# Sparse graph attention, four layers: another place for the sums of the weights and for the outputs of a block

## The chip, the cores and the metric

The kernel runs on one core of one Trainium2 chip. The metric is the device time of one execution in microseconds. The kernel before took 2802.78 us, the median of three runs (2800.01 to 2805.45).

The core's engines work side by side, each through its own instructions in order: TensorE (PE; its weight loads are listed apart as PEld), VectorE (DVE), ScalarE (ACT), GpSimd (POOL) and SyncE (SP). They wait for each other on semaphores. Transfers run on 16 DMA engines.

## The reference, cut to what matters

There are 8 batches of 2048 nodes with 128 features, and one adjacency matrix in which a node has some 16 neighbours. Layers 0 and 1 are attention with 8 heads of 16 features over the neighbours, an output projection, a layer norm, a feed-forward part and a second layer norm. Layers 2 and 3 are graph attention with one score for each pair.

```python
scores = jnp.einsum('bnhd,bmhd->bhnm', Q, K) / sqrt(HEAD_DIM)
attn = softmax(where(adj == 0, -inf, scores))          # layers 0 and 1
x = layer_norm(h + einsum('bhnm,bmhd->bnhd', attn, V) @ Wo + bo)
x = layer_norm(x + relu(x @ W1 + b1) @ W2 + b2)
...
e = leaky_relu(s_i[:, :, None] + s_j[:, None, :])      # layers 2 and 3
x = layer_norm(softmax(where(adj == 0, -inf, e)) @ h + x)
```

The change touches layers 0 and 1 alone. The softmax is computed there as a sum of exponentials times values (the accumulator) and a sum of the exponentials themselves; the division comes at the end of a block.

## The kernel before, in words

**Blocks and chunks.** The nodes are sorted by their number of neighbours and cut into 16 blocks of 128. Block t has at most `CAPS[t]` neighbours for each node, from 29 down to 10. All 8 batches are done at once. In layers 0 and 1 a chunk is two neighbours of all 128 nodes (one, where the number is odd), so a block has between 15 and 5 chunks. A chunk's rows (keys and values of 8 batches, 8 KB for each neighbour) are gathered by indirect DMA (line 302, issued by POOL, up to five chunks ahead) into one of seven buffers `kv`.

**One attention chunk** (`attention_chunk`, lines 629 to 683) is a generator with these steps:

1. DVE multiplies the keys by the query (L637).
2. DVE adds the two halves of that product (L643); PE transposes and sums it into scores (L316, tile `pair`); ACT takes the exponential (L659, tile `ring`).
3. PE transposes it back (L663) and ACT copies it as the weights (L667). For the last chunk of a block PE also sums all of the block's exponentials (`block_sums`, L616 and L621) and ACT copies the sums (`partial`, L626).
4. DVE multiplies the values by the weights (L675).
5. PE adds the first neighbour's product into the accumulator `acc` (L316), 8 matmuls.
6. The same for the second neighbour.

**The order of the work** is written out by hand in `layers` (lines 1243 to 1304). Iteration i does step 3 of chunk i-1 and step 6 of chunk i-3; steps 1 and 2 of chunk i, each followed by a `slot`; then `weigh`, which does steps 4 and 5 of chunk i-2; and a third slot. So DVE's order in one iteration is L637 of chunk i, slot, L643 of chunk i, slot, L675 of chunk i-2, slot. At the change from layer 1 to layer 2 all chunks that are still open are weighed in the first iteration of layer 2.

**A slot** advances every generator in `threads` by one step, then every one in `tails`, and issues further gathers if their conditions hold. From layer 1 on, while a layer's input table isn't complete, it advances the tails twice.

**The end of a block.** In `weigh`, when the chunk is the block's last, `sums` (L685 to L697) runs: DVE adds the two halves of the partial sums (L688, 128x64), ACT takes the logarithm (L690), and a thread `scales` is added, in which ACT takes the exponential of minus the logarithm (L710, 128x1024), PE transposes it in two halves in the next two slots (L719, recorded as L316 with tile `m`), and ACT copies each half into the tile `scale` (L721). For a layer's last block DVE also reduces all sums to a minimum and a maximum there (L694, L695). One iteration later, after step 6 of the last chunk, the thread `tail` (L1206) is added: it waits some slots, then `outputs` (L699 to L703) lets DVE multiply the accumulator by the scale in two halves into the tile `o`. After that two generators `attention_tail` (L728) are added to `tails`, one for each half of the batches: the output projection (L739, L743), layer norm (L483, L490), feed-forward part (L756, L761, L768, L773), second layer norm, and the projection of the next layer's rows (L520, L526 or L530). A whole tail takes 21 steps. It ends in `state_done` (L545): the block's state is stored and a later one loaded (SP, L551 and L298), and the rows are scattered into the next layer's table (POOL, L507). Gathers of the next layer wait for these scatters; the first two blocks of a layer have their neighbours sorted so that their first chunks don't need the last three blocks.

In layer 0 there is besides a thread `find_lists` for each block, started in the first iteration of the block two before: its DVE part (MAX8 and MATCH_REPLACE8, lines 361 to 398) makes the neighbour list of a block.

Of the kernel before, what the change touches and what calls it, by code (L numbers as in the profile page):

```python
# [20 lines left out]
NT = N // P  # L21
# [68 lines left out]
def sparse_path(ctx: ExitStack, tc: tile.TileContext, ins: dict, out: bass.AP, flag: bass.AP):  # L90
# [365 lines left out]
    def reciprocal_sums(l, t, w, columns, folded):  # L456

        sums = small.tile([P, columns], F32, tag="sums", name="sums")
        n = CAPS[t] if t > 0 else BASE
        nc.vector.tensor_reduce(  # L460
            sums, w[:, :n, :].rearrange("p s c -> p c s"), axis=AX.X, op=ALU.add
        )
        if t == 0:
            nc.vector.tensor_add(sums, sums, folded)
        nc.vector.tensor_reduce(dmin[:, l, t : t + 1], sums, axis=AX.X, op=ALU.min)
        nc.vector.tensor_reduce(dmax[:, l, t : t + 1], sums, axis=AX.X, op=ALU.max)
        nc.vector.reciprocal(sums, sums)
        return sums
# [216 lines left out]
    def sums(l, t, box):  # L685
        if l < 2:
            both = box["partial"]
            nc.vector.tensor_add(block_sum[:, t, :], both[:, : NB * NH], both[:, NB * NH :])  # L688
            box["r"] = small.tile([P, NB * NH], F32, tag="logs", name="logs", bufs=1)
            nc.scalar.activation(box["r"], block_sum[:, t, :], AF.Ln)  # L690
            threads.append(scales(l, box))
            if t == NT - 1:
                every = block_sum.rearrange("p t c -> p (t c)")
                nc.vector.tensor_reduce(dmin[:, l, :1], every, axis=AX.X, op=ALU.min)  # L694
                nc.vector.tensor_reduce(dmax[:, l, :1], every, axis=AX.X, op=ALU.max)  # L695
            return
        box["r"] = reciprocal_sums(l, t, box["w"], NB, box.get("folded"))  # L697

    def outputs(l, t, box):  # L699
        acc, scale = box["acc"], box["scale"]  # L700
        box["o"] = o = work.tile([P, NB, P], F32, tag="o", name="o", bufs=1)
        for i in range(0, NB, 4):
            nc.vector.tensor_mul(o[:, i : i + 4, :], acc[:, i : i + 4, :], scale[:, i : i + 4, :])  # L703

    def scales(l, box):

        box["scale"] = scale = work.tile([P, NB, P], F32, tag="oT", name="scale", bufs=1)
        if l < 2:
            r = box["r"].rearrange("p (b h) -> p b h", h=NH)
            nc.scalar.activation(  # L710
                scale.rearrange("p b (j h) -> p b j h", h=NH),
                r[:, :, None, :].to_broadcast([P, NB, HD, NH]), AF.Exp, scale=-1.0,
            )
            yield
        for i in range(0, NB, 4):
            pt = misc()
            for j in range(4):
                r = box["r"][:, i + j : i + j + 1].to_broadcast([P, P])
                turn_into(pt[:, j * P : (j + 1) * P], scale[:, i + j, :] if l < 2 else r, j == 0)  # L719
            yield  # L720
            nc.scalar.copy(scale[:, i : i + 4, :].rearrange("p b n -> p (b n)"), pt)  # L721
# [479 lines left out]
    def later(n, make):  # L1201
        for _ in range(n):
            yield
        yield from make()

    def tail(l, t, box):  # L1206
        for _ in range(4 if l < 2 else 3 if t > NT - 4 else 5):
            yield
        outputs(l, t, box)
        if l < 2:  # L1210
            tails.append(later(1, lambda: attention_tail(l, t, box, 0)))
            tails.append(later(4, lambda: attention_tail(l, t, box, 4)))
        else:
            tails.append(later(1, lambda: gat_tail(l, t, box)))
        yield
# [14 lines left out]
    def go(c, times=1):  # L1230

        for _ in range(times if c["l"] is not None else 0):
            next(c["run"], None)

    def weigh(some, added):

        for c2 in some:
            if c2["last"]:
                sums(c2["l"], c2["t"], c2["box"])
            go(c2, 2)  # L1240
            added.append(c2)

    def layers():
# [7 lines left out]
        for i in range(len(every) + 2):  # L1251
# [3 lines left out]
            while added:  # L1255
                c2 = added.pop(0)
                go(c2)
                if c2["last"]:
                    threads.append(tail(c2["l"], c2["t"], c2["box"]))
# [23 lines left out]
            if c["l"] not in (0, 1) and weighed:  # L1283
                weigh(weighed, added)
                weighed = []
# [9 lines left out]
            if len(weighed) > 2:  # L1295
                weigh(weighed[:1], added)
                weighed.pop(0)
            if c1["l"] in (2, 3):
                go(c1, 2)
                if c1["last"]:  # L1300
                    threads.append(tail(c1["l"], c1["t"], c1["box"]))
# [533 lines left out]
```

## Time and profile before

| what | value |
|---|---|
| runs | 2802.78 us median (2800.01 to 2805.45) |
| the profiled execution's own time | 2808.35 us |
| its span | 2806.6 us |
| granted TensorE clock, mean | 0.937 |
| busy: PE / PEld / DVE / ACT / POOL | 84% / 76% / 90% / 49% / 63% |
| DMA | 982 MB, 350 GB/s; gathers take 82% of 16 engines' span |
| attention layers (first gathered chunk to the entry of layer 2) | 245 to 1893 us of the span |
| L637, L643, L675 for two neighbours | 2.28, 1.22, 2.28 us |
| L688, pair of L703 | 0.22, 1.28 us |

The span runs from the first to the last recorded instruction; the own time is some 1.75 us longer. A row of the timeline gives the start (us), the duration (us), the engine, the line, the operation, the tile written and the tiles read with their shape, how many instructions were merged, and in brackets how long the engine had been idle and which instruction released it. In the list of waits the columns are the waiting engine, tile and line, what it waited for, the total in us, the number of times and the longest. Where a helper records every operation, all have one line: L316 is every transpose and every value sum, and the tile tells which (`pair` scores, `acc` values, `m` the rest).

### The profile page before, as it was taken

What the parts mean: (1) busy time and instruction counts of PE and PEld (TensorE: products, weight loads), DVE (VectorE), ACT (ScalarE), POOL (GpSimd) and SP (SyncE); (2) the same over time, 40 slices, a digit from 0 to 9 for tenths busy, and PEclk for the clock granted to TensorE, in tenths of its full rate; (3) what the DMA queues carried; (4) which work ended last, traced back from release to release, by engine and by line L of the source; (5) the groups of instructions that cost most, each with busy time, mean ns of one, the idle gap of its engine ahead of it and who ended that gap; (6) DMA issues with size and microseconds to landing.
All of it is one profiled execution on the core that took longest, in us unless ns stands there. A gap on an engine that the chain in (4) does not pass through costs nothing.

```text
span 2806.6 us, 48937 instructions
## 1 busy us (share of the span) xinstructions
PE 2349.6 (84%) x17811; PEld 2130.1 (76%) x17811; DVE 2513.9 (90%) x2467; ACT 1381.9 (49%) x5032; POOL 1774.4 (63%) x1346
## 2 busy tenths in 40 slices
PE   5866898898899998798989999997767887788885
PEld 4655787787788887688878888886667786787785
DVE  9697999999999887999999999985989997799895
ACT  3611444454555665154445555565445565445554
POOL 3377788778656455546565665573776775677772
PEclk9978999999999999999999999999788888999997
DMA  9898899999989888789999999985999998999994
GB/s 368 274 370 318 358 335 331 386 334 363 382 325 365 326 329 317 304 311 367 357 386 367 354 378 363 355 324 175 382 412 385 401 409 332 349 411 413 400 413 166
DMA packets 197730, 982.02 MB, mean 350 GB/s; under 512 B 30268, under 2 KB 32060, under 8 KB 125488
## 3 DMA queue, kind: packets, MB, share of 16 engines
q0 software_dynamic: 172080, 885.06, 82.0%
q1 hardware_dynamic: 20650, 68.39, 6.3%
q10 hardware_dynamic: 4752, 25.36, 2.7%
q8 instruction: 143, 2.34, 0.3%
q14 instruction: 105, 0.86, 0.1%
HBM read 921.28 MB, written 91.55 MB: 361 GB/s over the span
## 4 chain that ended last, share of the span: by engine, by line
PE 37%; DVE 27%; DMA 15%; issue 10%; ACT 8%; POOL 2%; POOLq 0%; ACTq 0%; DVEq 0%
PE acc L316 13%; DMA kv<-table,lists 11%; DVE kv L675 9%; DVE kv L637 8%; PE pair L316 4%; PE m L773 3%; PE m L756 3%; DVE kv L818 3%; PE m L520 2%; PE m L323 2%; PE m L768 2%; PE m L573 2%; PE m L739 1%; PE m L743 1%; POOL kv L302 1%
## 5 line engine op out<-in xcount | busy, mean ns | idle before, releaser
L302 POOL DMA_INDIRECT kv<-table,lists x938 | 1305.5, 1392 | 669.3 <-PE acc L316 288.0
L316 PE MATMUL acc<-ident,kv 128*128 128x128 f32 x8048 | 1059.2, 286 | 166.5 <-DVE kv L675 90.3
L316 PEld LDWEIGHTS acc<-ident,kv 128*128 128x128 f32 x8048 | 964.3, 148 | 230.0 <-DVE kv L675 114.4
L637 DVE TENSOR_TENSOR kv<-kv,q 128x2048 f32<-128x2048 f32 (+1 forms) x280 | 617.9, 2207 | 37.2 <-DMA kv<-table,lists 26.6
L675 DVE TENSOR_TENSOR kv<-kv,weights 128x2048 f32<-128x2048 f32 (+1 forms) x282 | 625.9, 2220 | 25.1 <-ACT weights L667 24.8
L818 DVE TENSOR_TENSOR kv<-kv,pair 128x3584 f32<-128x3584 f32 (+1 forms) x150 | 530.7, 3538 | 1.0
L316 PE MATMUL pair<-ident,kv 128*128 128x128 f32 (+1 forms) x2256 | 300.2, 277 | 87.4 <-issue 75.4
L643 DVE TENSOR_TENSOR kv<-kv 128x1024 f32<-128x1024 f32 (+1 forms) x282 | 334.9, 1187 | 9.2
L316 PEld LDWEIGHTS pair<-ident,kv 128*128 128x128 f32 (+1 forms) x2256 | 255.8, 140 | 107.8 <-issue 88.3
L302 POOL DMA_INDIRECT kv<-table,sorted_lists x150 | 195.7, 1304 | 139.2 <-PE acc L316 40.8
L659 ACT ACTIVATE ring<-pair 128x128 f32<-128x128 f32 (+1 forms) x282 | 77.7, 276 | 366.5 <-PE pair L316 302.2
L823 ACT ACTIVATE kv<-kv,ws 128x128 f32<-128x128 f32 x544 | 174.7, 397 | 153.3 <-DVE ws L812 144.0
L667 ACT COPY weights<-pair 128x128 f32<-128x128 f32 (+1 forms) x282 | 73.3, 260 | 357.1 <-PE pair L663 351.4
L483 ACT ACTIVATE n<-m,eps 128x128 f32<-128x128 f32 x512 | 181.6, 371 | 135.0 <-PE m L773 130.7
L860 ACT ACTIVATE n<-m,eps 128x128 f32<-128x128 f32 x256 | 90.8, 374 | 182.2 <-PE m L852 180.0
L773 PE MATMUL m<-w_L_w,hT 128*128 128x128 f32 x1024 | 156.4, 275 | 0.0
L490 ACT ACTIVATE n<-m,rs 128x128 f32<-128x128 f32 x512 | 146.4, 376 | 0.3
L773 PEld LDWEIGHTS m<-w_L_w,hT 128*128 128x128 f32 x1024 | 135.1, 192 | 0.0
L756 PE MATMUL m<-n1T,w_L_gnn_W 128*128 128x512 f32 x256 | 132.5, 602 | 3.0 <-ACT hT L761 1.8
L703 DVE TENSOR_TENSOR o<-acc,scale 128x512 f32<-128x512 f32 x128 | 83.2, 683 | 50.5 <-ACT scale L721 27.0
L520 PE MATMUL m<-w_L_h,xT 128*128 128x130 f32 x512 | 84.8, 298 | 46.5 <-ACT xT L494 29.3
L323 PE MATMUL m<-ident,n 128*128 128x128 f32 x640 | 113.4, 290 | 11.9 <-ACT n L490 5.6
(233 smaller groups left out, 3593.2 us busy)
## 6 DMA issues: line engine op xcount, KB each, us to landing
kept<-xT SPq DMA_DIRECT2D x48, 512.0 KB, 6.7
xT<-kept SPq DMA_DIRECT2D x48, 512.0 KB, 7.0
kv<-in_adj_dram SPq DMA_DIRECT2D x16, 1024.0 KB, 15.8
table<-kv ACTq DMA_DIRECT2D x16, 1024.0 KB, 4.5
kv<-table,lists POOLq DMA_INDIRECT x938, 8.8
kv<-in_x_nodes_dram ACTq DMA_DIRECT2D x16, 512.0 KB, 11.1
kv<-table,sorted_lists POOLq DMA_INDIRECT x150, 6.7
found<-kv POOLq DMA_DIRECT2D x16, 64.0 KB, 5.6
```

The costliest lines, as they stand in the source:

```text
L302: this = nc.gpsimd.indirect_dma_start(out=dst, out_offset=None, in_=tables[l][:, :] if need == NT else views[l][0], in_offset=bass.Indirec ...
L316: nc.tensor.matmul(dst, src, ident, start=start, stop=True, is_transpose=True, skip_group_check=True)
L323: nc.tensor.transpose(pt[:, j * P : (j + 1) * P], src[:, j, :], ident)
L483: nc.scalar.activation(dst[:, i, :], z[:, i, :], AF.Square, bias=eps, scale=D**-0.5, accum_out=ss[:, i : i + 1],)
L490: nc.scalar.mul(dst[:, i, :], z[:, i, :], rs[:, i : i + 1])
L637: nc.vector.tensor_mul(kk, kk, q[:, None].to_broadcast([P, ns, NB, D]))
L643: nc.vector.tensor_add(hk.rearrange("p j (c h) -> p c j h", h=NH), kj[:, :, :NH, :], kj[:, :, NH:, :])
L675: nc.vector.tensor_mul(vv, vv, w.rearrange("p (s b h) -> p (s b) h", b=NB, h=NH)[:, :, None, :] .to_broadcast([P, ns * NB, HD, NH]),)
L756: nc.tensor.matmul(ph, wt["1"][:, f * P : (f + 1) * P], n1T.rearrange("p b c -> p (b c)"), start=True, stop=True,)
L773: nc.tensor.matmul(y[:, j, :], hT[:, f, j, :], wt["2"][:, f, :], start=False, stop=f == 1, skip_group_check=True,)
L818: nc.vector.tensor_mul(hv[:, :, :nv, :], hv[:, :, :nv, :], wc[:, :, :nv, None].to_broadcast([P, ns, nv, D]))
L823: nc.scalar.mul(hv[:, i, b, :], hv[:, i, b, :], ws[:, i, b - nv : b - nv + 1])
```

## The change

For layers 0 and 1 the thread `tail` waits six slots in place of four before the outputs. And `weigh` calls `sums` for a last chunk of these layers after steps 4 and 5 of that chunk (the product L675 and the first neighbour's sums) and not ahead of them. `scales` still takes its first step in the slot that follows `weigh`. Layers 2 and 3 call `sums` elsewhere, and nothing changes in them.

```diff
     def tail(l, t, box):
-        for _ in range(4 if l < 2 else 3 if t > NT - 4 else 5):
+        for _ in range(6 if l < 2 else 3 if t > NT - 4 else 5):
             yield
         outputs(l, t, box)
...
     def weigh(some, added):

         for c2 in some:
-            if c2["last"]:
+            if c2["last"] and c2["l"] > 1:
                 sums(c2["l"], c2["t"], c2["box"])
             go(c2, 2)
+            if c2["last"] and c2["l"] < 2:
+                sums(c2["l"], c2["t"], c2["box"])
             added.append(c2)
```

So the outputs, which stood in the second slot of the second iteration after the sums (behind L643, ahead of L675), stand in the first slot of the third (behind L637, ahead of L643), and the whole tail with them two slots later. Where the blocks end at the entry of layer 2, the same count of slots holds.

## The prediction

> **What bounds the kernel now.** I read the busy table by stage first, then DVE's waits, then single blocks in the timeline, and last the boundary to layer 2. The attention layers lie at 245 to 1893 us of the span. The columns of the stage table are: stretch and its length, busy us of PE, PEld, DVE, ACT, POOL with instruction counts, the granted clock, the DMA share, GB/s.
>
> ```profile
> 245.00:760.00 515.00, 441.82 (x3355) 396.35 (x3356) 485.37 (x406) 231.75 (x791) 399.15 (x241) 0.96 0.93 357
> 760.00:1060.00 300.00, 287.00 (x2206) 254.54 (x2205) 272.53 (x195) 176.96 (x614) 165.99 (x101) 0.99 0.90 338
> 1240.00:1600.00 360.00, 327.10 (x2544) 294.32 (x2543) 348.11 (x205) 177.63 (x672) 212.37 (x127) 0.96 0.94 367
> 1600.00:1885.00 285.00, 271.64 (x2200) 245.76 (x2198) 268.71 (x164) 167.40 (x637) 174.28 (x104) 0.99 0.93 353
> ```
>
> In the first, long blocks of each layer DVE is the limit (94% and 97% busy, DMA close behind). In the later, short blocks there are more tails for each chunk, and PE is the limit (96% and 95%). So a DVE wait is worth something only where PE later sits idle for want of DVE. DVE's own waits in 245 to 1893:
>
> ```profile
> DVE o L703 <- ACT scale L721: 27.0, 19, 9.9
> DVE kv L675 <- ACT weights L667: 24.8, 15, 5.2
> DVE kv L637 <- DMA kv<-table,lists: 23.6, 13, 6.8
> DVE block_sum L688 <- ACT partial L626: 15.8, 11, 3.3
> ```
>
> The first and the last of them are the two instructions that the change moves: the outputs (L703) and the add of the halves (L688). One late block in the timeline:
>
> ```profile
> 892.12 1.22 DVE L643 TENSOR_TENSOR kv<-kv 128x1024 f32<-128x1024 f32 x1
> ...
> 895.03 0.69 DVE L703 TENSOR_TENSOR o<-acc,scale 128x512 f32<-128x512 f32 x1 [1.69 <-ACT scale L721]
> ...
> 895.36 0.62 ACT L721 COPY scale<-m 128x512 f32<-128x512 f32 x1
> ...
> 896.01 0.69 DVE L703 TENSOR_TENSOR o<-acc,scale 128x512 f32<-128x512 f32 x1 [0.29 <-ACT scale L721]
> 896.62 2.28 DVE L675 TENSOR_TENSOR kv<-kv,weights 128x2048 f32<-128x2048 f32 x1
> ...
> 905.99 0.33 PE L316 MATMUL acc<-ident,kv 128*128 128x128 f32 x1 [1.10 <-DVE kv L675]
> ```
>
> DVE stands 1.69 + 0.29 us before the outputs until ACT has copied the scale, works on without a break, and 11 us later PE stands 1.10 us for a product (L675) that is late.
>
> **The outputs, two slots later.** No instruction is added or taken away; all 32 pairs (1.2 us each) stay on DVE. They move from behind the tree add (L643), past one value product L675 (2.2 us) and one query product L637 (2.2 us). Here they would start at 893.3 + 4.4 = 897.7, and the second copy ends at 895.98, so the wait goes. What is late next is PE, so I take per block the smaller of DVE's wait and of the PE idle on DVE in the 14 us behind it: 800: min(1.19, 2.59) = 1.19; 850: 1.19; 895: min(1.98, 1.10) = 1.10; 940: 1.11; 985 and 1022: PE has no idle on DVE, 0; 1232: none, 0; 1752: min(0.61, 1.07) = 0.61; 1794: 0.71; 1837: min(0.71, 0.32) = 0.32; 1874: 0. Sum **-6.2**. In the other attention blocks the outputs do not wait, DVE runs without a gap, and moving 1.2 us inside it gives 0: it takes 1.2 us from the gap ahead of PE's value sums and puts it ahead of PE's score transposes.
>
> The longest wait, 9.9 us at 1068 (last block of layer 0), is bounded by 0 and -10.2. PE is filled by the tails there (59.75 of 65 us in 1040 to 1105), and behind 1068 its next gap over 0.2 us is 0.96, on ACT. I take 0.
>
> **The granted clock** adds to a PE gap. After the 2.29 us gap that the outputs cause at 1356.98 the stages read:
>
> ```profile
> 1355.00:1358.00 3.00, 1.02 (x9) 1.01 (x10) 3.00 (x2) 0.01 (x1) 0.00 (x0) 1.00 1.00 423
> 1358.00:1360.00 2.00, 2.00 (x11) 1.91 (x10) 1.97 (x2) 0.00 (x0) 1.65 (x1) 0.51 1.01 422
> ```
>
> The last column but two is the clock: 0.51. It stands at 0.64 in the next 2 us, and at 0.72 for 6 us in 812 to 818, behind the gaps of the block at 800. There it costs 6 x 0.28 = 1.7 us on PE. With 1.19 of that block's 2.59 us of gaps gone I take half of it, **-0.8** (bounds 0 and -1.7).
>
> The Trainium skill, "TensorE: Matmul & The Clock Gate", Part 1, says that the array drops to half clock after an idle window of about 3.4 us. That rule speaks against the change in layer 0, where the list search (MAX8 and the rest at 901.02 to 902.5, 1.5 us) shares its slot with the new place of the outputs: a gap of 1.0 + 1.2 + 1.5 = 3.7 us ahead of the score transposes. By the rule I estimate half of 3.4 us lost for each of some ten DVE-limited blocks, +17 us of PE time, yet in stretches where PE has room; the row above shows that 2.3 us are already enough, so the drop is paid there today, and the sum would not change by either.
>
> **The tail behind the outputs** moves with them, with everything it issues: the state's store and the load of a later state on SP (L551, L298), and the scatter of the rows on POOL (L507, 1.03 us each). A loaded state is used more than 15 chunks later; SP has nothing else queued. On POOL the gathers stand behind the scatter in order; inside a layer that is only another place for it. At the start of layer 1 the first gather that needs the last block's rows is that of chunk 14, issued some 2.5 chunks after the scatter, so 0. At the start of layer 2 it is chunk 7, and there it is on the path:
>
> ```profile
> 1949.37 1.03 POOL L507 DMA_INDIRECT table<-rows,perm  x1 [13.68 <-ACT own L543]
> ...
> 1956.11 1.02 POOL L302 DMA_INDIRECT kv<-table,lists  x1 [5.71 <-DMA table<-rows,perm]
> ...
> 1963.87 0.18 DVE L806 TENSOR_TENSOR kv<-kv,mine 128x16 f32<-128x16 f32 x1 [14.52 <-DMA kv<-table,lists]
> ```
>
> DVE idles 14.5 us until those rows are back. The tail there advances two steps a slot, and two slots are 2/3 of a chunk; the chunk pitch is 9.0 us (L818 starts at 1911.41 and 1920.43), so the upper bound is **+6.0**. The lower: PE begins the tail's first product only at 1917.45, 7.5 us after the outputs ended (1909.9), because it is behind; what is put ahead of it is one chunk's value sums, 24 matmuls that take 2.6 us (1911.91 to 1914.53). I take +2.6, then set against it the next part.
>
> **The halves, behind the value product.** Again nothing is added: 32 adds of 0.22 us. The add no longer holds the product up while the partial sums are late; the product needs the weights copy (L667), which ends 0.17 us (789, 839, 1606, 1654, 1700) to 1.07 us earlier than the partial copy. From the DVE starts this frees 5.0 of the 15.8 us, in blocks where PE is the limit and the outputs' wait would have swallowed it: 0. The exception is the entry into layer 2:
>
> ```profile
> 1888.80 0.22 DVE L688 TENSOR_TENSOR block_sum<-partial 128x64 f32<-128x64 f32 x1 [3.28 <-ACT partial L626]
> ...
> 1891.32 2.28 DVE L675 TENSOR_TENSOR kv<-kv,weights 128x2048 f32<-128x2048 f32 x1
> ...
> 1893.66 1.76 PE L316 MATMUL acc<-ident,kv 128*128 128x128 f32 x8 [3.45 <-DVE kv L675]
> ```
>
> There the add and two reductions (1.22 + 1.21) stand ahead of the product, and PE waits 3.45 us. The weights are there at 1888.23, so the product starts 3.1 us earlier. ACT pays: its logarithm (L690) now waits for an add at about 1890.5 instead of 1888.8, and the tail's n1T (L494) queued behind it ends at 1892.8; PE's next product L756 then starts at 1892.8, not 1895.21: -2.4. Bounds -3.1 and 0; I take -1.6, between ends that are close. With the +2.6 above the boundary is **+1.0**.
>
> The new wait elsewhere: ACT's logarithm now waits for the product too (2.2 us, 1.13 for a one-neighbour chunk). Behind it in ACT's queue are the scale's exponential and the next weights copy. In the DVE-limited blocks the logarithm ran at 1343.38, 1.4 us behind the add; it would run 1.1 us later, the exponential would end at 1345.8, and the copy due at 1345.66 moves by 0.15 against a product that starts at 1347.75: hidden. In late blocks ACT reaches the logarithm 6 to 9 us after the add anyway: 0.
>
> **Sum.** -6.2 - 0.8 + 1.0 = **-6.0 us**. The profiled execution took 2808.35 (span 2806.6 and 1.75 around it), which becomes 2802.4; that execution is 5.6 above the median of the runs, 2802.78, so the forecast is 2802.8 - 6.0 = **2797**.
>
> **Rivals.**
> *More is won.* If PE's fullness is itself made by late products, all of the waits are paid back: 27.0 - 10.2 = 16.8 at the outputs and 5.0 at the adds, less the +1.0: -20.8, 2782. For it: the clock falls after gaps, so a removed gap returns more than itself. Against: at 985, 1022 and 1232 PE has no idle on DVE to give back.
> *Nothing is won.* PE at 95 to 96% is the limit, the removed DVE wait returns one product later at L675 <- ACT weights (2.07 us at 932), and the boundary's +1.0 remains less 2 for odd gaps: about -1, 2802.
> *Slower: the rows of the last attention block come late.* Place: the start of layer 2, the scatter L507 and the gather of chunk 7. Price: the full 2/3 of a chunk, +6.0, with nothing won in the late blocks: 2809. It decides once the boundary costs over 5.6 us more than the blocks give. For it: DVE idles 14.5 us on exactly this chain. Against: PE was 7.5 us behind the outputs there.
>
> **How the numbers follow.** About 0.2% (5.6 us) is what a measurement of this kernel can tell from no change. Forecast case 0.46, its own range 2792 to 2802, as its bounds give: 0.28 faster and 0.18 same. More won 0.20, faster. Nothing won 0.10, same. Late rows 0.24: 0.22 slower, 0.02 same. Faster 0.48, same 0.30, slower 0.22. The range 2782 to 2811 reaches from the larger gain to the late rows with a little above them.
>
> **What would show it.** Right: the wait L703 <- ACT scale falls from 27.0 to a few us; the waits of L688 on L626 nearly vanish; PE's idle on L675 behind the late blocks shrinks by about 6 us; 760 to 1060 gets some 4 to 5 us shorter; 1240 to 1600 keeps its length. Wrong: the wait on L667 or on PE's buffers m grows by what L703 loses; the gap ahead of chunk 7 of layer 2 grows from 14.5 to about 20; the score transposes in DVE-limited blocks start to hold DVE.

## The result, and the profile after

The changed kernel takes 2878.73 us, the median of five runs (2877.09 to 2882.93); the kernel before, run beside it, 2801.57 us. The ratio is 1.0282, 95% interval 1.0271 to 1.0294: 77 us slower. The profiled execution took 2878.73 us as well, with a span of 2876.9 us.

Where it was lost can be read from DVE's rows of L688, of which there is one for each block. I take the first and the last of each attention layer as marks ("the layers" below means the two middle stretches, 1492.9 us before and 1561.7 us after):

| stretch, us of the profiled execution | before | after |
|---|---|---|
| start to the first sum of layer 0 | 254.4 | 256.1 |
| layer 0, first to last sum | 787.5 | 819.3 |
| to the first sum of layer 1 | 141.5 | 141.4 |
| layer 1, first to last sum | 705.4 | 742.4 |
| to the end of the span | 917.8 | 917.7 |

So the loss, 68.8 of the 70.3 us between the spans, lies inside the two layers and is spread over them: some 2.3 us for each of the 30 steps from block to block. It isn't at an entry into a layer.

The stage table for these two stretches, first of before, then of after (stretch and its length, busy us of PE, PEld, DVE, ACT, POOL with instruction counts, granted clock, DMA share, GB/s):

```profile
254.00:1042.00 788.00, 707.80 (x5427) 634.07 (x5428) 735.66 (x588) 396.10 (x1358) 550.59 (x336) 0.97 0.93 352
1183.00:1889.00 706.00, 652.38 (x5156) 588.18 (x5157) 668.50 (x403) 374.26 (x1414) 414.14 (x249) 0.98 0.93 355
```

```profile
256.00:1075.00 819.00, 722.41 (x5409) 640.21 (x5409) 735.98 (x587) 393.30 (x1357) 524.27 (x333) 0.96 0.89 338
1217.00:1959.00 742.00, 655.19 (x5136) 585.64 (x5136) 667.59 (x401) 371.33 (x1410) 405.81 (x250) 0.98 0.89 338
```

DVE and ACT are busy for the same time as before, the DMA share falls, PE is busy 17 us longer. No engine got more instructions; they wait for each other. DVE's waits in the whole execution of the kernel after:

```profile
DVE kv L675 <- ACT weights L667: 108.5, 46, 7.1
...
DVE kv L637 <- ACT q L578: 40.3, 15, 4.5
...
DVE o L703 <- ACT scale L721: 13.8, 8, 3.9
DVE kv L637 <- DMA kv<-table,lists: 11.7, 7, 5.3
```

The wait of the outputs on the scale is halved (27.0 before; 9.8 us of the 13.8 lie ahead of layer 2), that of L688 on L626 is gone from the list (15.8 before), as meant. But the value product now waits 108.5 us for the copy of the weights (24.8 before), and the query product 40.3 us for the queries (6.8 before). Both are copies by ACT, an engine that is busy half of the time. On PE, the sum of its idle time in the layers that a DVE instruction ended fell from 68.7 to 16.6 us, and that which an ACT instruction ended rose from 17.2 to 93.0 us. A third part, for which the profile names no releaser ("issue"), rose from 48.7 to 71.5 us. All of it stands ahead of score transposes, and each time it ends 0.1 us after a tree add, so it too is PE waiting for DVE. Before, and after with the outputs and a part of the list search ahead of the add:

```profile
339.02 1.22 DVE L643 TENSOR_TENSOR kv<-kv 128x1024 f32<-128x1024 f32 x1
...
340.35 1.06 PE L316 MATMUL pair<-ident,kv 128*128 128x128 f32 x8 [1.54 <-issue]
```

```profile
348.37 1.27 DVE L703 TENSOR_TENSOR o<-acc,scale 128x512 f32<-128x512 f32 x2
349.55 1.22 DVE L643 TENSOR_TENSOR kv<-kv 128x1024 f32<-128x1024 f32 x1
...
350.87 1.53 PE L316 MATMUL pair<-ident,kv 128*128 128x128 f32 x8 [4.13 <-issue]
```

So PE's waits for DVE fell by some 29 us in all, and its waits for ACT rose by 76.

One slot shows how. First the kernel before, in a late block of layer 0, one iteration with two tails in it:

```profile
917.30 1.04 PE L316 MATMUL pair<-ident,kv 128*64 128x128 f32 x8
...
918.44 0.49 PE L768 MATMUL m<-center,n1T 128*128 128x128 f32 x2
918.55 0.27 ACT L659 ACTIVATE ring<-pair 64x128 f32<-64x128 f32 x1 [0.39 <-PE pair L652]
...
923.91 0.27 PE L663 MATMUL pair<-ident,ring 64*128 64x64 f32 x1
...
924.22 0.21 ACT L667 COPY weights<-pair 128x64 f32<-128x64 f32 x1 [0.24 <-PE pair L663]
...
925.39 1.15 ACT L490 ACTIVATE n<-m,rs 128x128 f32<-128x128 f32 x4
...
926.40 0.72 ACT L761 ACTIVATE hT<-m,w_L_col 128x512 f32<-128x512 f32 x1
```

PE does the score transposes (tile `pair`) first and the feed-forward product y (L768, L773) behind them; ACT copies the weights (L667) as soon as PE has them, and the norm's scaling (L490) and the second relu (L761) come after the copy. Then the same part of the kernel after, in the iteration behind the sum of that block:

```profile
944.88 0.61 PE L773 MATMUL m<-w_L_w,hT 128*128 128x128 f32 x4
...
945.32 1.02 PE L756 MATMUL m<-n1T,w_L_gnn_W 128*128 128x512 f32 x2
...
946.18 1.04 PE L316 MATMUL pair<-ident,kv 128*128 128x128 f32 x8
...
947.26 0.28 ACT L659 ACTIVATE ring<-pair 128x128 f32<-128x128 f32 x1 [5.17 <-PE pair L316]
...
948.79 0.27 PE L663 MATMUL pair<-ident,ring 128*128 128x128 f32 x1
...
949.31 0.67 ACT L761 ACTIVATE hT<-m,w_L_col 128x512 f32<-128x512 f32 x1
949.88 1.13 ACT L490 ACTIVATE n<-m,rs 128x128 f32<-128x128 f32 x4
...
950.88 0.71 ACT L761 ACTIVATE hT<-m,w_L_col 128x512 f32<-128x512 f32 x1
...
951.45 0.30 ACT L667 COPY weights<-pair 128x128 f32<-128x128 f32 x1
...
951.78 2.29 DVE L675 TENSOR_TENSOR kv<-kv,weights 128x2048 f32<-128x2048 f32 x1 [3.75 <-ACT weights L667]
```

Now y and the first feed-forward product stand ahead of the score transposes. ACT has nothing for 5.17 us, and then everything at once: the exponential, the norm's squares, a relu, the scaling, another relu. PE has transposed the weights back at 949.06; the copy stands at the end of that queue and starts at 951.45, 2.4 us later, and DVE idles 3.75 us. In the kernel after, DVE waits of 3.0 to 3.8 us on this copy return at most of the late blocks (644, 702, 814, 864, 952 us and on).

That slot shows who stands in line, not what each place costs. PE's own waits on ACT, in the whole execution, before and after, say more:

```profile
PE m L316 <- ACT scale L710: 8.9, 15, 2.0
PE m L323 <- ACT n L490: 5.6, 7, 2.5
PE m L756 <- ACT hT L761: 1.8, 1, 1.8
PE pair L316 <- ACT weights L667: 1.6, 4, 0.7
```

```profile
PE m L316 <- ACT scale L710: 25.0, 23, 2.3
PE m L323 <- ACT n L490: 19.3, 27, 3.4
PE m L573 <- ACT q L578: 11.1, 13, 0.9
PE m L756 <- ACT hT L761: 7.7, 6, 1.3
PE pair L316 <- ACT weights L667: 5.2, 13, 0.7
```

Most of PE's idle time on ACT stands ahead of products into the tile `m`, those of the tails, of the queries and of the scale: 82 of 94 us in the layers (gaps of any length counted), 14 of 18 before. The chunk's own products are held up behind them: summed over the 244 chunks in the layers, the score transposes start 1106 us after the end of the tree add that they need, 716 us before.

### The profile page after: what moved, and what is told of

It is laid out like the page before. It is cut to its first block, busy times and chain, and to the rows that moved or that the text cites. A ratio compares the mean times of both kernels' runs of the same rounds, so it can differ in the third digit from the quotient of the medians.

```text
span 2876.9 us, 48906 instructions
## 1 busy us (share of the span) xinstructions
PE 2361.9 (82%) x17811; PEld 2128.8 (74%) x17811; DVE 2512.9 (87%) x2467; ACT 1377.1 (48%) x5032; POOL 1733.3 (60%) x1346
## 5 line engine op out<-in xcount | busy, mean ns | idle before, releaser
L302 POOL DMA_INDIRECT kv<-table,lists x938 | 1258.6, 1342 | 745.0 <-PE acc L316 269.6
L316 PE MATMUL acc<-ident,kv 128*128 128x128 f32 x8048 | 1046.5, 284 | 116.9 <-DVE kv L829 45.8
L675 DVE TENSOR_TENSOR kv<-kv,weights 128x2048 f32<-128x2048 f32 (+1 forms) x282 | 627.0, 2223 | 108.5 <-ACT weights L667 108.5
L637 DVE TENSOR_TENSOR kv<-kv,q 128x2048 f32<-128x2048 f32 (+1 forms) x280 | 618.0, 2207 | 55.2 <-ACT q L578 40.3
L316 PE MATMUL pair<-ident,kv 128*128 128x128 f32 (+1 forms) x2256 | 306.2, 280 | 124.0 <-issue 103.5
L643 DVE TENSOR_TENSOR kv<-kv 128x1024 f32<-128x1024 f32 (+1 forms) x282 | 334.7, 1187 | 8.6
L302 POOL DMA_INDIRECT kv<-table,sorted_lists x150 | 187.9, 1253 | 152.1 <-PE acc L316 60.4
L773 PE MATMUL m<-w_L_w,hT 128*128 128x128 f32 x1024 | 160.1, 279 | 1.5 <-ACT hT L761 1.5
L507 POOL DMA_INDIRECT table<-rows,perm x57 | 92.5, 1622 | 92.5 <-ACT own L543 50.0
L490 ACT ACTIVATE n<-m,rs 128x128 f32<-128x128 f32 x512 | 146.0, 373 | 0.8
L773 PEld LDWEIGHTS m<-w_L_w,hT 128*128 128x128 f32 x1024 | 138.2, 195 | 2.0 <-ACT hT L761 1.9
L667 ACT COPY weights<-pair 128x128 f32<-128x128 f32 (+1 forms) x282 | 74.1, 263 | 131.0 <-PE pair L663 127.6
L323 PEld LDWEIGHTS m<-ident,n 128*128 128x128 f32 x640 | 79.7, 145 | 67.5 <-ACT n L490 30.7
## 6 DMA issues: line engine op xcount, KB each, us to landing
kv<-in_x_nodes_dram ACTq DMA_DIRECT2D x16, 512.0 KB, 12.8
```

The source lines that it names most:

```text
L302: this = nc.gpsimd.indirect_dma_start(out=dst, out_offset=None, in_=tables[l][:, :] if need == NT else views[l][0], in_offset=bass.Indirec ...
L316: nc.tensor.matmul(dst, src, ident, start=start, stop=True, is_transpose=True, skip_group_check=True)
L323: nc.tensor.transpose(pt[:, j * P : (j + 1) * P], src[:, j, :], ident)
L490: nc.scalar.mul(dst[:, i, :], z[:, i, :], rs[:, i : i + 1])
L637: nc.vector.tensor_mul(kk, kk, q[:, None].to_broadcast([P, ns, NB, D]))
L643: nc.vector.tensor_add(hk.rearrange("p j (c h) -> p c j h", h=NH), kj[:, :, :NH, :], kj[:, :, NH:, :])
```

## The experiments

**Slots.** An iteration has three slots. Slot 1 lies between the query product L637 and the tree add L643; behind it come the score transposes and the exponential. Slot 2 lies between these and the value product L675, slot 3 behind that, ahead of the next iteration's copy L667. A tail takes one step a slot, so two slots more put each of its steps, in both of its halves (they start three slots apart), from slot s to s + 2, or s - 1 of the next iteration:

| step | engine | before | after |
|---|---|---|---|
| z; squares; scaling; transposes; eviction (first norm) | PE; ACT; ACT; PE; ACT | 3; 1; 2; 3; 1 | 2; 3; 1; 2; 3 |
| first half of the feed-forward's first product | PE | 2 | 1 |
| its relu, and the second half | ACT, PE | 3 | 2 |
| second relu | ACT | 1 | 3 |
| y | PE | 2 | 1 |
| second norm: squares; scaling | ACT | 3; 1 | 2; 3 |
| transposes; their eviction | PE; ACT | 2; 3 | 1; 2 |
| projection: two products; last copy | PE; ACT | 1, 2; 3 | 3, 1; 2 |

**Theories.** The first is that these places cost the 69 us (slots in steps of three are the same, so seven slots should cost nothing). The rivals: the add behind the product does it; the lateness of the outputs and of the rows does it; the outputs' new place on DVE, ahead of the tree add, does it. All diffs are against the changed kernel. "Sums in front" means that `sums` is called ahead of the product, as before. Where a time for "the layers" is given, it is from the one profiled execution.

**One part alone, and other counts of slots.** `e1_sums_only`, `e2_late_only`, `e3_seven` and `e5_phase_back` ran beside the kernel before at 2800.95 us, `e4_five` beside it at 2892.74 us on another chip.

The sums behind the product, the outputs after four slots (`e1_sums_only`):

```diff
-        for _ in range(6 if l < 2 else 3 if t > NT - 4 else 5):
+        for _ in range(4 if l < 2 else 3 if t > NT - 4 else 5):
```

> The halves added behind the value product, the outputs at four slots as before. Theory P (phase: with two more slots the tail's steps fall into other slots of an iteration, and what they put on PE and ACT then stands ahead of the score transposes and of the weights copy): within 5 us of the kernel before, the wait of L675 on L667 near 25 us. Rival S (the moved add makes ACT's logarithm wait for the product, and the weights copies behind it are late): most of the 77 us, with the wait of L675 on L667 near 100. Rival L (lateness: the whole tail runs into the next block's start): like P.

Measured: 2801.56 us, ratio 0.9993 (0.9982 to 1.0003). The layers take 1485.6 us. The sums' place costs nothing. (The layers are 7.3 us shorter than before, in one execution of each; so much isn't told apart by them.)

The other part, six slots and sums in front (`e2_late_only`):

> The outputs at six slots, the halves added ahead of the value product as before. P: 2870 to 2885, the whole loss. S: within 10 us of the kernel before. L: the whole loss as well.

Measured: 2881.11 us, ratio 1.028 (1.0262 to 1.0299), the layers 1555.6 us. The whole loss is in the count of slots.

Seven slots, sums in front (`e3_seven`, `range(7 if l < 2 ...`):

> The outputs at seven slots, so a whole chunk later than before, the halves as before. P: seven is four plus a whole iteration of three slots, every step is back in its slot: 2790 to 2815. L: later still, so 2890 to 2920. S: within 10 us of before, but then the run with six slots alone is too.

Measured: 2810.78 us, ratio 1.0027 (1.0013 to 1.0041), the layers 1484.3 us. Later still, and the layers are 8.6 us shorter than before: lateness isn't the cause. The 0.27% are lost outside of them: 3.0 us on the way to the first sum of layer 1, 7.6 behind the last sum of layer 1.

Five slots, sums in front (`e4_five`):

> The outputs at five slots, the halves as before: the third of the three phases. The tail's matmuls in the first slot are then the output projection (2.0 us a half), the transposes (0.5) and half of the first feed-forward product (1.0): 3.5 us, against 1.0 at four slots and some 5 at six. PE: between the two, in proportion 2801 + 77 x 2.5 / 4 = 2850, 2825 to 2865. A theory of lateness: a third to a half of the loss, 2825 to 2840, which this run alone doesn't tell apart; the run with seven slots did.

Measured: 2941.32 us, ratio 1.0146 (1.0089 to 1.0202), the layers 1515.1 us. So the three places give 1492.9 (four slots), 1515.1 (five), 1555.6 (six) and 1484.3 us (seven). On its chip the run with five lost 48.6 us in all, more than these 22.2.

**Outputs and tails apart.** Outputs after six slots, sums in front, and the tails one slot later, so that their steps are back in the old slots (`e5_phase_back`):

```diff
-            tails.append(later(1, lambda: attention_tail(l, t, box, 0)))
-            tails.append(later(4, lambda: attention_tail(l, t, box, 4)))
+            tails.append(later(2, lambda: attention_tail(l, t, box, 0)))
+            tails.append(later(5, lambda: attention_tail(l, t, box, 4)))
```

> The outputs at six slots, and one more slot between them and the tail, so that the outputs alone have moved in DVE's order and the tail's steps are in their old slots, a chunk later. P: 2790 to 2820. A rival O (the place of the outputs on DVE, ahead of the tree add and so of the score transposes, is what costs): 2850 to 2880. L: 2880 and over.

Measured: 2802.97 us, ratio 1.0007 (0.9995 to 1.0018), the layers 1480.1 us. The outputs' place on DVE is innocent: the layers are 12.8 us shorter, and the entry into layer 1 gives 8.6 of it back (150.1 us for 141.5). How much of the 12.8 comes from the new place isn't shown, as the layers of `e3_seven`, where the outputs stand in the old slot a chunk later, are 8.6 us shorter. PE's idle time behind the products fell from 68.7 to 36.5 us, that behind the tree adds rose from 48.7 to 67.9: most of the gap was moved, not removed.

The reverse: outputs after four slots, the tails two slots later (`e6_tails_late`, `later(3, ...)` and `later(6, ...)`), sums in front:

> The outputs and the halves as before; only the two generators of the tail start two slots later. If the loss is the phase of the tail's steps on PE and ACT alone: the whole of it, ratio 1.022 to 1.033, and from the first to the last add of halves of each attention layer some 32 and 37 us more than before (787 and 705). If the outputs' place on DVE has a part in it: half or less.

Measured: 3018.65 us beside 2905.43 for the kernel before on that chip, ratio 1.0397 (1.0358 to 1.0435), the layers 1588.8 us. The tail's steps alone lose more than the change does, 96 us in the layers. DVE waits 91.2 us for the scale there, and 13.8 in the changed kernel, so with late tails the outputs' new place spares a wait; that this is the difference between 96 and 69 us is argued, not tried.

**Single steps moved, and none of them the cause by itself.** From the rows of one block I took y ahead of the score transposes for the cause, then the squares ahead of the copy, then any work in slot 1. The three ran beside the kernel before at 2892.74 us. First y one slot later, its squares in the same slot (`e7_y_behind`):

```diff
         yield
+        yield
         y = misc().rearrange("p (b c) -> p b c", c=D)
...
-        yield from normed(y, n2)
+        yield from normed(y, n2, False)
```

where the new argument leaves out the slot ahead of the squares.

> The changed kernel, but the second feed-forward product of the tail (L768 and L773, 12 matmuls for a half, 2.6 us) is issued one slot later, so behind the score transposes on PE and not ahead of them; its squares and all that follows stay in their slots. Theory PE (what costs is tail matmuls ahead of the score transposes: scores, exponential, weights copy and the query's copy come late): 50 to 75 of the 77 us come back, 2802 to 2830, and both DVE waits (L675 on L667, 108 us; L637 on L578, 40 us) fall by more than half. Theory ACT (the first norm's squares ahead of the weights copy on ACT): under 15 us come back.

Measured: 2987.82 us, ratio 1.0301 (1.0236 to 1.0366), the layers 1556.0 us: nothing came back.

The first norm's squares and its scaling together in slot 1, behind the copy (`e8_squares_behind`; in `normed`, for the first norm, the `yield` moves from behind the squares to ahead of them):

> The changed kernel, but the first norm's squares (L483, L473, L474, some 1.9 us a half) are issued one slot later, together with the scaling L490, so behind the weights copy on ACT and not ahead of it; the rest stays in its slot. PE: 0 to 15 us come back, 2863 to 2880. ACT: 50 us and more, under 2830.

Measured: 3009.05 us, ratio 1.0395 (1.0335 to 1.0455), the layers 1590.6 us: worse. No step of a tail in slot 1 and two in slot 2 (`e9_empty_slot`; `slot` gets the number of turns as an argument, 0 and 2 there in layers 0 and 1):

> The changed kernel, but in attention chunks the first slot (between the query product and the tree add) takes no step of a tail and the second takes two, so no tail matmul at all stands ahead of the score transposes. PE: at least as much as the run with the second feed-forward product alone, 2790 to 2820. ACT: under 15 us come back, 2863 and over.

Measured: 2989.94 us, ratio 1.0314 (1.0259 to 1.037), the layers 1570.8 us. All three theories of one guilty step fell. Nor does the lateness of the copy by itself go with the loss: the time from the end of the transposes back (L663) to the start of the copy, summed over the layers, is 49 us before and 179 after, but 127 us both in `e8_squares_behind` and in `e16_from_ph1` below, whose layers take 1590.6 and 1469.4 us.

**Which half of the tail.** Both with sums in front and outputs after four slots, beside the kernel before at 2905.43 us. The tail up to the first norm in the late slots, the rest in the old ones (`e10_front`, tails at `later(3, ...)`, `later(6, ...)`, and one slot more):

```diff
         affine(n1T, pt, wt["col"][:, 0:2])
         yield
+        yield
```

> The tail's first part (output projection, first norm, transposes) starts two slots later, as in the changed kernel, and one more slot behind it brings the second part (feed-forward, second norm, projection) back into its old slots, a chunk later. If the first part's phase costs (first squares ahead of the weights copy): 60% of the loss and more, ratio over 1.017. If the second part's does: under 1.010.

Measured: 2900.26 us, ratio 0.9981 (0.9956 to 1.0006), the layers 1472.2 us. They are 20.7 us shorter than before, with the outputs in their old place. The reverse, the first part in the old slots and two slots more at the same place (`e11_back`):

> The first part in its old slots, and the second part (feed-forward, second norm, projection) two slots later. If the second part's phase costs: ratio over 1.017. If the first part's does: under 1.010. If both runs give about half, or neither gives much, it is the two together, a fixed order of all steps against the chunk's own.

Measured: 3007.04 us, ratio 1.0358 (1.032 to 1.0395), the layers 1585.3 us. The loss is in the second part, from the feed-forward on.

**The staircase.** Four kernels, beside the kernel before at 2799.26 us, are the changed kernel with one slot more in the second part, at one place after the other; all steps from there on are back in their old slots. A fifth, beside it at 2800.92 us, fills the largest step. The diff is always the same line (under a condition where the place is in a loop or in a helper that both norms share):

```diff
+        yield
```

ahead of the second half of the feed-forward's first product (`e16`), ahead of y (`e13`), between the second norm's squares and scaling (`e14`), between its scaling and the transposes (`e17`), ahead of `project` (`e15`).

> The changed kernel with one more slot ahead of the second half of the feed-forward's first product: only that part's first product and first relu stay in the late slots, all from there on is back in the slots of before. If the loss comes from y, the second norm or the projection: layers 0 and 1 together within 10 us of before's 1493 us, wait of the query product on q near 7 us. If it comes from the first product and relu: still near 1560 us, as in the changed kernel (819.3 and 742.4).

> The changed kernel with one more slot ahead of y: both products of the feed-forward's first layer and both relus stay in the late slots, y, the second norm and the projection are back. If the loss comes from y or what follows it: layers 0 and 1 together near 1493 us. If it comes from the second relu in the slot ahead of the weights' copy: still near 1560 us. A value in between would say that it is a sum of several steps.

> The changed kernel with one more slot between the second norm's squares and its scaling: y and the squares stay in the late slots (y ahead of the score transposes), the scaling, the transposes back, their eviction and the projection are in the slots of before. If the loss is in the scaling ahead of the weights' copy, or in the projection: layers 0 and 1 together near 1493 us. If y and its squares are what costs: still near 1560 us, though moving y alone (an earlier run) gave nothing back.

> The changed kernel with one more slot ahead of the projection: all up to the second norm's eviction stays in the late slots, only the projection's products and copies are in the slots of before. If the projection's first product and its eviction in the late slots cost: layers 0 and 1 together near 1493 us. If anything ahead of it does: near 1560 us. If several steps each cost a part, the four kernels make a staircase from 1493 to 1560 us in the order in which they return the steps.

> The changed kernel with one more slot between the second norm's scaling and its transposes: y, the squares and the scaling (ScalarE, ahead of the weights' copy) stay in the late slots, the transposes (TensorE), their eviction and the projection are back. If the transposes ahead of the score transposes cost the 55 us: layers 0 and 1 together near 1511 us, as with the slot ahead of the scaling, and 2835 us in all. If the scaling ahead of the weights' copy costs them: near 1566 us and 2880 us in all.

| back in the old slots | the layers, us | PE idle there until ACT, us | time, us | ratio (95%) |
|---|---|---|---|---|
| nothing (the changed kernel) | 1561.7 | 93.0 | 2878.73 | 1.0282 (1.0271 to 1.0294) |
| projection (`e15`) | 1565.9 | 90.0 | 2879.85 | 1.0282 (1.0244 to 1.0319) |
| from the transposes on (`e17`) | 1541.1 | 78.7 | 2865.11 | 1.0246 (1.0222 to 1.0271) |
| from the scaling on (`e14`) | 1511.0 | 62.3 | 2835.41 | 1.0127 (1.0091 to 1.0162) |
| from y on (`e13`) | 1476.5 | 42.9 | 2815.86 | 1.0052 (1.0032 to 1.0073) |
| from the second half of the first product on (`e16`) | 1469.4 | 32.2 | 2798.48 | 0.9999 (0.9984 to 1.0014) |

There is no single guilty step. The projection is free; the transposes and their eviction account for 25 us of the layers, the scaling 30, y and its squares 35, the second half of the first product with the second relu 7. These lengths are of one execution each; by the times of the runs the same steps are 15, 30, 20 and 17 us. PE's idle time until ACT falls at every step. For the transposes the waits of PE name a part of the mechanism. In `e15`, where they stand in slot 1, the next slot behind the scaling in slot 3 (total, times, longest, in the whole execution):

```profile
PE m L323 <- ACT n L490: 26.8, 39, 3.0
```

and in `e17`, one slot later:

```profile
PE m L323 <- ACT n L490: 4.6, 6, 1.5
```

Of these 22 us, 15.4 lie in the layers (15.7 and 0.3), but PE's whole idle time until ACT fell by 11.3 there, so this wait is a part of the step and not all of it. The staircase also says why `e7` gave nothing back: it moved y behind the score transposes, but left the squares that wait for it and the scaling ahead of the copy, so the chain from y to the scaling had only become tighter. That last is argued, not tried.

**What is better than both.** Several kernels whose tails run later have shorter layers, and the later rows of a layer's last blocks give it back at the entries (146.9 us into layer 1 in `e16`). So the last two blocks of each layer keep the old places. First with the tails one slot later as in `e5_phase_back`, sums behind (`e12_better`):

```diff
-        for _ in range(6 if l < 2 else 3 if t > NT - 4 else 5):
+        for _ in range((6 if t < NT - 2 else 4) if l < 2 else 3 if t > NT - 4 else 5):
...
-            tails.append(later(1, lambda: attention_tail(l, t, box, 0)))
-            tails.append(later(4, lambda: attention_tail(l, t, box, 4)))
+            tails.append(later(2 if t < NT - 2 else 1, lambda: attention_tail(l, t, box, 0)))
+            tails.append(later(5 if t < NT - 2 else 4, lambda: attention_tail(l, t, box, 4)))
```

> For all but the last two blocks of a layer the outputs at six slots with the tail in its old slots (as in the run that did this for all blocks, where the two layers lost 9 and 4 us but the entry into layer 1 gained 9), for the last two blocks everything at four; the halves behind the product. Phase theory: 2785 to 2797 where before runs at 2801, ratio 0.994 to 0.998. A rival that the later tail costs at the entries whatever the last two blocks do: 0.999 to 1.002.

Measured: 2896.7 us beside 2905.43, ratio 0.9974 (0.995 to 0.9997), barely faster, the layers 1484.9 us. Then with the slot of `e16` in its place (`e18_mid_blocks`):

```diff
         for f in range(2):
+            if f == 1 and t < NT - 2:
+                yield
             ph = misc()
...
-        for _ in range(6 if l < 2 else 3 if t > NT - 4 else 5):
+        for _ in range((6 if t < NT - 2 else 4) if l < 2 else 3 if t > NT - 4 else 5):
```

> The changed kernel with one more slot ahead of the second half of the feed-forward's first product, but in the last two blocks of each attention layer the outputs after four slots and no slot more, as before. If what the earlier kernel with that slot gained in the layers (1469 us for both against 1493) was given back by the later rows of the last blocks: layers near 1475 us, entry into layer 1 near 141 us, 2780 to 2790 us in all, 0.4 to 0.7 per cent faster than before. If it was given back in layers 2 and 3 for another reason: within 0.2 per cent of before.

Measured: 2783.36 us beside 2800.92, ratio 0.9944 (0.9932 to 0.9957): 17.6 us faster than before. The layers take 1473.7 us, the entry into layer 1 140.9 us (146.9 in `e16`), the stretch behind the layers 911.0 us (924.9). Its DVE waits:

```profile
DVE kv L675 <- ACT weights L667: 39.7, 24, 5.2
...
DVE o L703 <- ACT scale L721: 20.9, 5, 9.9
...
DVE kv L637 <- ACT q L578: 14.8, 10, 2.5
```

The copy of the weights is still later than before (39.7 against 24.8 us), but PE's idle time in the layers that DVE's products ended is 13.8 us, against 68.7 before; that behind the tree adds is 72.8 (48.7 before), that until ACT 34.0 (17.2). Which of the moves wins the 19 us of the layers isn't shown: `e18` has the outputs and the tail's first part in late slots, and on one and the same chip `e10_front`, with the first part alone in late slots, takes 1472.2 us in the layers, and `e12`, with the outputs alone, 1484.9. The kernel of `e10` with the last two blocks left alone was not tried.

## Why the prediction was wrong

The forecast was 2797 us, with 2811 as its upper end; the time is 2878.73. By its steps:

- **The step that failed: "The tail behind the outputs moves with them", priced at 0.** I looked at the tail's DMAs alone, the store, the load and the scatter (inside a layer "only another place for it"), and inside the layers none of them mattered. What I left out are its 21 steps on PE and ACT, which got other neighbours in both queues. Measured: about +96 us in the layers when they alone move (`e6_tails_late`), +69 together with the rest of the change. `e1_sums_only`, `e3_seven` and `e5_phase_back` take the rivals away, `e10_front` and `e11_back` put the loss into the tail's second part, the staircase divides it.
- **The view that misled.** I wrote that a DVE wait is worth something only where PE later sits idle for want of DVE, and so read PE's idle time on DVE alone. PE's idle time on ACT was 17.2 us before, too small to look at; it became 93.0. ACT at 49% isn't the bound by its share, but its results come too late for PE all the same.
- **Outputs, -6.2.** The wait on the scale fell, ahead of layer 2 from 27.0 to 9.8 us, though not to the few us that I had forecast. What it is worth isn't shown. PE's waits for DVE fell by 29 us net, but in `e10_front`, whose outputs do not move, they are 19 us shorter too, and with the tail in its old slots the layers are 12.8 us shorter and the time is the same (`e5_phase_back`). The other half of the term, that moving 1.2 us "inside it gives 0", has the direction right: the gap ahead of the value sums went, that ahead of the score transposes grew, to 4.13 us in the row above.
- **Clock, -0.8.** Too small to be seen in the means of the layers: 0.97 and 0.98 in the two layers before, 0.96 and 0.98 after.
- **Entry into layer 2, +1.0** (+2.6 for late rows, -1.6 for the product first). Both terms were mis-sized. The rows of after:

```profile
1957.04 2.29 DVE L675 TENSOR_TENSOR kv<-kv,weights 128x2048 f32<-128x2048 f32 x1 [4.06 <-ACT weights L667]
1959.25 0.22 DVE L688 TENSOR_TENSOR block_sum<-partial 128x64 f32<-128x64 f32 x1
```

```profile
2026.78 1.03 POOL L507 DMA_INDIRECT table<-rows,perm  x1 [20.74 <-ACT own L543]
...
2040.23 0.18 DVE L806 TENSOR_TENSOR kv<-kv,mine 128x16 f32<-128x16 f32 x1 [20.41 <-DMA kv<-table,lists]
```

  The product stands ahead of the add, but it waited 4.06 us for its weights. PE's wait behind it did fall, from 3.45 to 1.28 us. DVE's gap ahead of chunk 7 went from 14.52 to 20.41 us: +5.9, the upper bound that I had worked out, not 2.6. In the sum some 2 us of it show: the stretch behind the last sum is as long as before (917.8 and 917.7 us), but it no longer holds the product of 2.3 us, which now stands ahead of this mark. With the last two blocks in the old places (`e18_mid_blocks`) the gap ahead of chunk 7 is 14.60 us, in `e16_from_ph1` 20.55.
- **The rival on the slower side** was this delay. It came with its price, but it is 5.9 us at one gap, against 68.8 in the layers. The true rival, new places of the tail's steps in the queues of PE and ACT, was not among mine, though one of my signs named its trace: that the wait on L667 or on PE's buffers `m` would grow. I had it grow by what L703 loses; the wait on L667 grew by 83.7 us.
- **Sums behind the product, 0, and the logarithm's later wait, 0.** Right (`e1_sums_only`).
- **The rule on the clock gate** that I weighed against the change decided nothing: no granted clock of a layer moved by more than 0.01. The drop is paid in both kernels: behind the gap of 4.13 us at 350.87 the granted clock is 0.61 and 0.53 in the next two stretches of 2 us, and before, behind a gap of 2.29 us at 343.70, 0.65 and 0.50.

The Trainium skill, "PSUM — Partial Sum Buffer", section "Engine vs sequencer instructions", says that ScalarE's queue is strictly first in, first out. The rows from 947.26 to 951.45 agree: the copy, which could start at 949.06, stands behind a relu, the scaling and another relu of the tails. The Trainium skill, "Perfetto Trace Analysis", section "Identifying the Most-Contended Engine", says that the most-contended engine is the one with the highest occupancy (TensorE and DMA are judged by other measures there), and to optimize it first. Here that is DVE with 90%, and its busy time in the layers is the same in both kernels (1403 and 1404 us): the loss shows in the waits, not in the busy time.

**Left open.** Of the 68.8 us in the layers, PE's idle time explains 46.5 (ACT +75.8, DVE's products -52.1, DVE's tree adds +22.8). PE's busy time grew by 17 us for the same products, and in `e16_from_ph1` it is 1348 us against 1360 before; a lower clock in short stretches would do that, but it wasn't separated. Which late result of ACT costs how much is not settled either: moving single steps gave nothing back, and the tails' steps wait for each other. The division of the staircase holds for one order of returning the steps; another order could divide it otherwise.

## What to carry to other kernels

When a thread that takes one step a slot is started some slots later, write down, for each of its steps, what now stands behind it in every engine's queue, above all short copies that another engine waits for; a shift by a whole iteration keeps these neighbours, a shift by part of one doesn't. As the staircase suggests, keep long chains of a background thread (product, squares, scaling, transposes) from standing ahead of a chunk's score transposes and the copy of its weights, however idle the engine is on average. If moving one instruction is worth something, move that alone and give its followers their old places back: that alone took the loss away here (`e5_phase_back`, the same time as before). With one more slot inside the tail and the last two blocks left alone the kernel went from 2.8% slower to 0.6% faster; how much of that gain belongs to the outputs isn't shown.

## What the runs showed of the hardware

Not expected: chips differ in the gather layers 2 and 3. The kernel before took about 2800 us on two chips, 2893 us on a third and 2905 us on a fourth. In the profiled executions the stretch behind the layers takes 911 to 933 us where the kernel before takes 2800, and 1013 to 1036 us on the other two, whichever the kernel. The stretch from 2100 to 2400 us, in these layers, whose code is the same in all kernels, first of the changed kernel, then of `e9_empty_slot`:

```profile
2100.00:2400.00 300.00, 239.03 (x1742) 224.82 (x1741) 286.83 (x337) 173.56 (x694) 228.34 (x205) 0.87 1.02 406
```

```profile
2100.00:2400.00 300.00, 223.71 (x1563) 208.08 (x1564) 254.09 (x290) 150.37 (x599) 201.22 (x182) 0.83 0.95 358
```

406 GB/s in one, 358 in the other. For that reason the times of each kernel are set against the kernel before on its own chip. The lengths of the attention layers are set against those of one execution of the kernel before; it has no profile on the two slower chips, where eight of the kernels of this text ran, and seven of these came out 9 to 32 us slower than the lengths of their layers say. So a small difference between these layers and those of before says little; the verdicts on these kernels rest on their ratios.
